# Loading and transposing the prefetched mask tiles earlier in a hand-ordered graph-attention kernel

## The chip, the cores and the metric

The kernel runs on one core of one Trainium2 chip, in one launch. The metric is device time in microseconds (us), as the median of several runs. TensorE (PE) does matmuls and transposes, VectorE (DVE) and ScalarE (ACT) work on whole tiles, GpSimd (POOL) adds tiles and issues the transfers that convert types or add into their destination, SyncE (SP) issues the other transfers. Each engine takes its instructions in the order of the program; an instruction that waits holds those behind it on the same engine.

## The reference, cut to what matters

For each of 16 samples (1024 nodes, 256 features) there are two attention layers over the same adjacency matrix, 4 heads of 64 in the first and 8 heads of 32 in the second:

```python
h = jnp.maximum(_layernorm(x), 0.0)
q, k, v = heads(h @ Wq), heads(h @ Wk), heads(h @ Wv)
scores = einsum('bhnd,bhmd->bhnm', q, k) / sqrt(D)
scores = where(adj > 0, scores, -inf)        # layer 1: adj == 0 gives -inf
x = x + (softmax(scores) @ v).reshape(b, n, e) @ Wo.T + bo
```

`adj` is int32 and has 16 x 1024 x 1024 entries of 0 or 1. The kernel computes scores transposed (keys on the partitions), so it needs the adjacency transposed too.

## The kernel before, in words

**Stream of steps.** Each sample is 16 steps of layer 0 and 32 of layer 1. The stream takes layer 0 of sample b + 1 and then layer 1 of sample b, over and over, so 48 steps bring one sample forward. In what follows `a` is the first step of layer 0 of sample b + 1 and `c` = a + 16 the first of layer 1 of sample b. A step computes four 128x512 blocks of scores (`scores`, L400, TensorE, into two PSUM pairs of which there are three), masks them (`exponentials`, L416, VectorE), exponentiates them (L421, ScalarE), and two steps later (`LEAD`) multiplies them with the values (`weigh`, L433, TensorE). If a step has a large item (keys, queries, values, the output projection), the `weigh` of an even step is put off to the next, and one does both.

**The mask.** `masks[b]` holds the transposed adjacency of a sample as fp8, in two halves of four tiles. A tile t (128 rows of the adjacency) takes three steps of its own:

- `load` (L128): GpSimd issues the transfer of 128x1024 int32 to bf16 into the tile `adj`. This tag has **one** buffer, so a load waits until the flip of the tile before has read it.
- `flip` (L134): SyncE issues a transposing transfer `adj` to `adjT`. That tag has one buffer as well, so a flip waits for the load and for the put of the tile before.
- `put` (L143): ScalarE converts `adjT` to the fp8 mask.

Layer 1 reads the same mask after `second` (L151) has changed its values in place.

**What sets the order.** All work beside the steps is given a due step by hand: `later(i, f, ...)`. Within a step the order is: scores, `weigh`, the counts and GpSimd adds of `count_steps`, the exponentials, the add tiles of layer 0, then the due items in the order in which they were registered, large ones last. The loads, flips and puts are registered before the stream runs, so they come before a spread, an invert or an accumulate that falls due in the same step, as those are registered while it runs.

For the masks of samples 2 to 15 the puts of tiles 0 to 7 are due at a + 7, 12, 17, 22, 33, 37, 41 and 45; tiles 2 to 7 thus fall into layer 1. For `masks[1]` a loop of its own spaces the tiles by two steps in the first layer 0. `masks[0]` goes through staging tiles and isn't touched.

**What GpSimd and SyncE have in layer 1.** The softmax sums of a group of 8 steps are made by adding probability tiles. At each odd step GpSimd adds the tile of the step two back to the one before it (L534, 128x2048, 4.7 us); some of the results are added together by transfers with accumulation (`accumulate`, L520, 1 MB). In program order this gives, on GpSimd:

- a+31: L534; a+33: L520, L534; a+35: L534; a+36: L520; a+37: L534, L520; a+39: L534; a+41: L520, L534; a+43: L534; a+44: L520
- between them: `add_bias` (L198, x<-bo) at a+34 and a+43, the four small instructions of `stats` (L177 to L183) at a+38, `normalize` (L352) at a+42

The probability tiles of odd steps have two buffers: the masking of step i + 2 (VectorE, L416) waits for the L534 of step i, as that one reads the tile to be overwritten.

SyncE has for each group a `spread` (four issues of L333, sums<-s, after ScalarE's copy L320), and an `invert`: one issue of L343 (vd<-vn) and four of L346 (inv<-vd), which wait until L343's transfer has landed. In layer 1 the spread of a group that ended at step i is due at i + 8, the invert at i + 12, the `normalize` at i + 17 in the first half; groups end at a+25 and a+33, so there is a spread at a+33 and a+41 and an invert at a+37 and a+45.

Of the kernel before, what the change touches and what calls it, by code (L numbers as in the profile page):

```python
# [82 lines left out]
def fast_program(ctx, tc, a, w, loads, chk):  # L83
# [375 lines left out]
    class Stream:  # L459
# [12 lines left out]
        def later(self, i, f, *args):  # L472
            self.due.setdefault(i, []).append((f, args))
# [116 lines left out]
    mask, inp = masks[0], inputs[0][0]  # L590
# [74 lines left out]
    later = stream.later  # L665

    def norms(inp, half, *at):

        for i, f in zip(at, (inp.stats, inp.stats, inp.norm, inp.norm)):
            later(i, f, half, (0, 1) if i in (at[0], at[2]) else (2, 3))  # L670
        later(at[3] + 1, inp.add_bias, half)

    def half_inputs(inp, half, *at):

        for i, f in zip(at, (inp.turn, inp.k, inp.q, inp.values)):
            later(i, f, half)
# [3 lines left out]
        later((u - 4) // 2, flip, u)  # L680
        later(u - 1, mask.put, u)
    for t in range(NT):
        i = 6 + 2 * t
        later(i - 3, masks[1].load, t)
        later(i - 2, masks[1].flip, t)
        later(i, masks[1].put, t)
# [5 lines left out]
    for b in range(B - 1):  # L692
        mine, a, c = inputs[1][b], first[b + 1], second[b]
        if b == 0:

            norms(mine, 0, a + 5, a + 6, a + 8, a + 9)
            half_inputs(mine, 0, a + 11, a + 12, a + 14, a + 14)
            norms(mine, 1, a + 13, a + 14, a + 15, c)
            half_inputs(mine, 1, c + 1, c + 3, c + 6, c + 4)
        else:  # L700
            norms(mine, 0, a - 20, a - 19, a - 16, a - 15)
            half_inputs(mine, 0, a - 13, a, a + 2, a + 8)
            norms(mine, 1, a - 14, a - 10, a - 8, a - 6)
            half_inputs(mine, 1, a - 1, c, c + 6, c + 2)
        for i, u in zip((0, 2, 4, 6, 8, 10, 12, 13), range(NT)):
            later(a + i, masks[b].second, u)
        if b + 2 < B:
            other, mask = inputs[0][b + 2], masks[b + 2]
            later(a + 5, open_x, b + 2, 0)
            later(a + 13, open_x, b + 2, 1)  # L710
            if b == 0:
                norms(other, 0, a + 14, a + 15, c + 2, c + 3)
                half_inputs(other, 0, c + 5, c + 8, c + 16, c + 18)
                norms(other, 1, c + 3, c + 4, c + 6, c + 7)
                half_inputs(other, 1, c + 11, c + 22, c + 26, c + 30)
            else:
                norms(other, 0, a + 10, a + 12, a + 13, a + 15)
                half_inputs(other, 0, c + 1, c + 8, c + 16, c + 18)
                norms(other, 1, c, c + 4, c + 5, c + 6)
                half_inputs(other, 1, c + 9, c + 22, c + 26, c + 30)  # L720
            for i, t in zip((7, 12, 17, 22, 33, 37, 41, 45), range(NT)):
                later(a + i - 5 + (t > 4), mask.load, t)
                later(a + i - 2, mask.flip, t)
                later(a + i, mask.put, t)
        else:
            last, e = inputs[1][b + 1], c + 32
            norms(last, 0, c + 5, c + 6, c + 8, c + 9)
            half_inputs(last, 0, c + 11, c + 14, c + 16, c + 20)
            norms(last, 1, c + 13, c + 14, c + 16, c + 17)
            half_inputs(last, 1, c + 19, c + 24, e + 6, e + 4)  # L730
            for u in range(NT):
                later(c + 8 + 2 * u, masks[b + 1].second, u)
# [158 lines left out]
def kernel(  # L891
# [28 lines left out]
    with ExitStack() as fast, tc.manual_schedule():  # L920
        fast_program(fast, tc, a, w, loads, chk)
# [61 lines left out]
```

## Time and profile before

| | |
|---|---|
| median of 3 runs | 3354.03 us (3348.64 to 3355.82) |
| profiled execution | 3351.91 us, its span 3349.8 us |
| busy | PE 3254.1 us (97%), DVE 2530.3 (76%), POOL 2349.8 (70%), ACT 2172.9 (65%) |
| granted TensorE clock | 0.989 |
| transfers that GpSimd issues | q0: 224.42 MB, 37.6% of 16 engines' span |
| transfers that SyncE issues | q1: 104.41 MB, 13.8% |
| load of a mask tile | 256 KB read, 3.9 us to landing (median of 128) |
| flip of a mask tile | 4.1 us to landing (median of 124) |
| accumulate p<-p | 1024 KB, 8.5 us to landing (median of 150) |

How to read it: a line of the costliest groups gives the source line, the engine, the operation, the tiles by name (written <- read), their shapes and the number of instructions; then the busy time in us and the mean ns of one; then the idle time of that engine just before these instructions, and what ended most of it. A line of the waits gives who waited for whom, the total in us, how often, and the longest. A line of a timeline gives the start in us from the start of the span, the duration in us, engine, line, operation and tiles, the count of instructions merged into it, and in brackets the idle time before it and its releaser. Durations of issues on SP and of DMA lines on POOL are those of the issuing, not of the transfer.

### The profile page before, as it was taken

What the parts mean: (1) busy time and instruction counts of PE and PEld (TensorE: products, weight loads), DVE (VectorE), ACT (ScalarE), POOL (GpSimd) and SP (SyncE); (2) the same over time, 40 slices, a digit from 0 to 9 for tenths busy, and PEclk for the clock granted to TensorE, in tenths of its full rate; (3) what the DMA queues carried; (4) which work ended last, traced back from release to release, by engine and by line L of the source; (5) the groups of instructions that cost most, each with busy time, mean ns of one, the idle gap of its engine ahead of it and who ended that gap; (6) DMA issues with size and microseconds to landing.
All of it is one profiled execution on the core that took longest, in us unless ns stands there. A gap on an engine that the chain in (4) does not pass through costs nothing.

```text
span 3349.8 us, 44407 instructions
## 1 busy us (share of the span) xinstructions
PE 3254.1 (97%) x16990; PEld 1274.2 (38%) x16990; DVE 2530.3 (76%) x2760; ACT 2172.9 (65%) x2402; POOL 2349.8 (70%) x1244
## 2 busy tenths in 40 slices
PE   8999999999999999999999999999999999999898
PEld 3343343333334343343434334344343343433333
DVE  5777877778777787776877767777687876778866
ACT  5567576675756757567575766757667576674565
POOL 4578586775857858577686776858668586785766
PEclk9999999999999999999999999999999999999999
DMA  7338265472643827456274563836638365380431
GB/s 142 66 73 148 66 120 102 86 145 64 125 94 81 147 64 139 80 98 127 68 145 79 98 124 65 149 81 107 118 64 151 70 114 108 76 155 26 87 78 31
DMA packets 309453, 331.74 MB, mean 99 GB/s; under 512 B 189552, under 2 KB 257392, under 8 KB 290032
## 3 DMA queue, kind: packets, MB, share of 16 engines
q0 software_dynamic: 73824, 224.42, 37.6%
q1 hardware_dynamic: 235408, 104.41, 13.8%
q8 instruction: 135, 2.21, 0.3%
q14 instruction: 86, 0.70, 0.1%
HBM read 119.54 MB, written 17.56 MB: 41 GB/s over the span
## 4 chain that ended last, share of the span: by engine, by line
PE 81%; DMA 6%; POOL 5%; ACT 4%; DVE 3%; issue 2%; SPq 1%; ACTq 0%; POOLq 0%; DVEq 0%
PE ps L400 27%; PE po L433 25%; PE pq L225 11%; PE py L381 7%; PE pv L262 6%; PE pz L301 4%; POOL p L534 4%; DMA adjT<-adj 3%; ACT p L421 2%; DVE p L416 2%; DMA p<-p 2%; PE ph L208 1%; ACT mask L143 1%; ACT hT L209 0%; ACT s L320 0%
## 5 line engine op out<-in xcount | busy, mean ns | idle before, releaser
L416 DVE SCALAR_TENSOR_TENSOR p<-mask,ps 128x1024 f32<-128x1024 fp8e4 x1536 | 1794.4, 1214 | 646.4 <-PE ps L400 599.3
L421 ACT ACTIVATE p<-p 128x1024 f32<-128x1024 f32 x1536 | 1611.5, 1056 | 871.8 <-DVE p L416 829.8
L534 POOL TENSOR_TENSOR p<-p,p 128x2048 f32<-128x2048 f32 x255 | 1191.2, 4675 | 240.2 <-PE po L433 221.3
L400 PE MATMUL ps<-qT,kT 32*128 32x512 f32 (+1 forms) x6144 | 1165.0, 637 | 12.8 <-DVE p L416 11.3
L433 PE MATMUL po<-p,v 128*32 128x512 f32 (+1 forms) x6144 | 1016.4, 608 | 39.1 <-ACT p L421 38.1
L400 PEld LDWEIGHTS ps<-qT,kT 32*128 32x128 f32 (+1 forms) x6144 | 376.7, 186 | 695.9 <-issue 372.6
L446 POOL TENSOR_TENSOR p<-p 128x1024 f32<-128x1024 f32 x128 | 318.9, 2491 | 299.6 <-DVE p L445 294.6
L433 PEld LDWEIGHTS po<-p,v 128*32 128x32 f32 (+1 forms) x6144 | 231.8, 118 | 744.1 <-issue 515.5
L445 POOL TENSOR_TENSOR p<-p 128x1024 f32<-128x1024 f32 x64 | 151.5, 2368 | 250.2 <-DVE p L442 179.7
L262 PE MATMUL pv<-wv,hT 128*128 128x256 f32 x1024 | 238.9, 387 | 14.5 <-ACT hT L209 14.5
L225 PE MATMUL pq<-hT,wk 128*128 128x512 f32 x512 | 239.0, 610 | 1.5 <-ACT hT L209 1.3
L381 PE MATMUL py<-wo,cat 128*128 128x256 f32 x1008 | 234.9, 386 | 2.2 <-ACT hT L209 1.0
L225 PE MATMUL pq<-hT,wq 128*128 128x512 f32 x512 | 236.6, 605 | 0.1
L262 PEld LDWEIGHTS pv<-wv,hT 128*128 128x128 f32 x1024 | 190.3, 191 | 87.9 <-ACT hT L209 26.8
L381 PEld LDWEIGHTS py<-wo,cat 128*128 128x128 f32 x1008 | 187.5, 191 | 72.7 <-issue 45.5
L143 ACT ACTIVATE mask<-adjT,mhalf 128x1024 fp8e4<-128x1024 bf16 x124 | 140.7, 1136 | 92.7 <-DMA adjT<-adj 92.7
L520 POOL DMA_DIRECT2D p<-p x150 | 151.3, 1008 | 54.2 <-POOL p L534 21.6
L352 POOL TENSOR_TENSOR cat<-cat,inv 128x512 f32<-128x512 f32 x127 | 169.2, 1332 | 8.8 <-DMA inv<-vd 6.2
L301 PE MATMUL pz<-p,ones 128*32 128x512 f32 (+1 forms) x1112 | 172.7, 595 | 0.8 <-ACT s L320 0.8
L448 POOL TENSOR_TENSOR p<-p,p 128x1024 f32<-128x1024 f32 x64 | 156.1, 2439 | 5.0
L442 DVE TENSOR_TENSOR p<-p 128x1024 f32<-128x1024 f32 x128 | 156.0, 1219 | 0.0
L225 PEld LDWEIGHTS pq<-hT,wk 128*128 128x128 f32 x512 | 93.0, 191 | 143.5 <-issue 94.1
(50 smaller groups left out, 1697.2 us busy)
## 6 DMA issues: line engine op xcount, KB each, us to landing
p<-p POOLq DMA_DIRECT2D x150, 1024.0 KB, 8.5
adj<-in_adj_dram POOLq DMA_DIRECT2D x128, 256.0 KB, 3.9
x<-bo POOLq DMA_DIRECT2D x64, 512.0 KB, 5.7
x<-in_x_dram SPq DMA_DIRECT2D x32, 512.0 KB, 4.4
inv<-vd SPq DMA_DIRECT2D x128, 128.0 KB, 2.9
inv<-vd SPq DMA_DIRECT2D x252, 64.0 KB, 2.7
out_dram<-x SPq DMA_DIRECT2D x31, 512.0 KB, 3.0
sums<-s SPq DMA_DIRECT2D x384, 2.0 KB, 1.8
```

Of the source, the lines that this page charges most:

```text
L143: nc.scalar.activation(self.m[qh][:, :, ts(t % 4, P)], self.flipped.pop(t), AF.Identity, bias=w.mhalf[:, 0:1], saturate=False,)
L225: nc.tensor.matmul(pq[:, m, :], wt[self.layer][:, c, ts(m, P)], self.hT[half][:, c, :], start=(c == 0), stop=(c == 1),)
L262: nc.tensor.matmul(pv[:, i, :], self.hT[half][:, c, ts(i, P)], w.v[self.layer][:, c, :], start=(c == 0), stop=(c == 1),)
L301: nc.tensor.matmul(self.s[r * self.D : (r + 1) * self.D, :], w.ones[:, : self.D], p[:, r, :], start=start, stop=stop,)
L352: nc.gpsimd.tensor_mul(o, o, self.inv)
L381: nc.tensor.matmul(py[:, i, :], self.half.cat[:, c, ts(i, P)], w.o[self.layer][:, c, :], start=(c == 0), stop=(c == 1),)
L400: nc.tensor.matmul(st.ps[i // 2][:, i % 2, :], gr.inp.kT[r * D : (r + 1) * D, gr.g, ts(kt, P)], gr.inp.qT[gr.qh][r * D : (r + 1) * D, gr.g ...
L416: nc.vector.scalar_tensor_tensor(out=half, in0=gr.mask.m[gr.qh][:, kt, :].unsqueeze(1).to_broadcast([P, 2, 512]), scalar=BIG, in1=st.ps[i] ...
L421: nc.scalar.activation(half, half, AF.Exp, scale=gr.scale)
L433: nc.tensor.matmul(gr.o[r * D : (r + 1) * D, :], gr.inp.v[:, kt, h * D : (h + 1) * D], st.p[:, i, :], start=(kt == 0), stop=(kt == NT - 1),)
L446: nc.gpsimd.tensor_add(a, a, b)
L534: nc.gpsimd.tensor_add(one, one, st.p)
```

## The change

```diff
     for t in range(NT):
-        i = 6 + 2 * t
+        i = 5 + 2 * t
         later(i - 3, masks[1].load, t)
         later(i - 2, masks[1].flip, t)
         later(i, masks[1].put, t)
...
             for i, t in zip((7, 12, 17, 22, 33, 37, 41, 45), range(NT)):
-                later(a + i - 5 + (t > 4), mask.load, t)
-                later(a + i - 2, mask.flip, t)
+                later(a + i - 6, mask.load, t)
+                later(a + i - 3, mask.flip, t)
                 later(a + i, mask.put, t)
```

In the first loop all three items of each tile of `masks[1]` come one step earlier. In the second, the puts stay where they are. All flips come one step earlier: at a + 4, 9, 14, 19, 30, 34, 38 and 42. The loads of tiles 0 to 4 come one step earlier and those of tiles 5 to 7, which stood four steps ahead of their puts, two: at a + 1, 6, 11, 16, 27, 31, 35 and 39. No instruction is added or removed.

## The prediction

> **What bounds the kernel now.** I read the page first. TensorE is busy for 97% of the span, at a granted clock of 0.989, so the layers' matmuls set most of the time, and a change in the mask's transfers can only win back gaps. The waits say where a mask tile makes one:
>
> ```profile
> L143 ACT ACTIVATE mask<-adjT,mhalf 128x1024 fp8e4<-128x1024 bf16 x124 | 140.7, 1136 | 92.7 <-DMA adjT<-adj 92.7
> ```
> ```profile
> ACT mask L143 <- DMA adjT<-adj: 92.7, 16, 7.7
> POOL adj L128 <- DMA adjT<-adj: 61.3, 15, 5.5
> DVE p L416 <- POOL p L534: 45.9, 41, 4.8
> ```
>
> ScalarE writes 124 tiles but waits in 16 of them. Two of these waits (1.0 and 1.7 us in ScalarE's timeline) lie in the first 75 us. The other 14, (92.7 - 2.7)/14 = 6.4 us each, come once in each of the 14 samples whose masks the main loop prefetches (b + 2 = 2 to 15), and the chain in order of time has an adjT transfer of 6.4 to 9.5 us in every one. I looked at one, from 1718 to 1768 us. The order of the puts shows which tile it is: t = 6, put at a+41. GpSimd's and SyncE's timelines there:
>
> ```profile
> 1718.73 0.92 POOL L520 DMA_DIRECT2D p<-p  x1 [1.79 <-PE po L433]
> ...
> 1723.92 0.84 POOL L128 DMA_DIRECT2D adj<-in_adj_dram  x1
> 1724.52 1.60 POOL L198 DMA_DIRECT2D x<-bo  x1
> 1726.18 4.56 POOL L534 TENSOR_TENSOR p<-p,p 128x2048 f32<-128x2048 f32 x1
> 1730.69 0.88 POOL L520 DMA_DIRECT2D p<-p  x1
> 1731.30 4.87 POOL L534 TENSOR_TENSOR p<-p,p 128x2048 f32<-128x2048 f32 x1
> 1736.47 0.87 POOL L520 DMA_DIRECT2D p<-p  x1 [0.30 <-POOL p L534]
> 1737.05 0.86 POOL L128 DMA_DIRECT2D adj<-in_adj_dram  x1
> ...
> 1739.88 4.56 POOL L534 TENSOR_TENSOR p<-p,p 128x2048 f32<-128x2048 f32 x1
> 1745.19 0.92 POOL L520 DMA_DIRECT2D p<-p  x1 [0.75 <-PE po L433]
> 1745.88 4.79 POOL L534 TENSOR_TENSOR p<-p,p 128x2048 f32<-128x2048 f32 x1
> 1754.50 0.60 POOL L128 DMA_DIRECT2D adj<-in_adj_dram  x1 [3.82 <-DMA adjT<-adj]
> 1755.11 1.29 POOL L352 TENSOR_TENSOR cat<-cat,inv 128x512 f32<-128x512 f32 x1
> 1756.36 4.57 POOL L534 TENSOR_TENSOR p<-p,p 128x2048 f32<-128x2048 f32 x1
> ```
> ```profile
> 1723.23 3.00 SPq L333 DMA_DIRECT2D sums<-s  x4
> 1728.24 2.30 SPq L134 DMA_TRANSPOSE adjT<-adj  x1
> ...
> 1738.93 3.77 SPq L346 DMA_DIRECT2D inv<-vd  x4
> 1746.22 2.05 SPq L134 DMA_TRANSPOSE adjT<-adj  x1
> ```
> ```profile
> 1753.96 1.15 ACT L143 ACTIVATE mask<-adjT,mhalf 128x1024 fp8e4<-128x1024 bf16 x1 [5.71 <-DMA adjT<-adj]
> ```
> ```profile
> 1760.96 2.35 DVE L416 SCALAR_TENSOR_TENSOR p<-mask,ps 128x1024 f32<-128x1024 fp8e4 x2 [4.00 <-POOL p L534]
> ```
>
> Load 6 goes out right behind a 1 MB accumulate (L520, 1736.47) and lands 9.1 us later. Its flip starts at 1746.22, now right behind the next accumulate (1745.19), and takes 7.7 us, to 1753.94. ScalarE was ready for the put at 1748.25. There is one adj buffer, so GpSimd sits in load 7 until the same flip lands, which holds its next two large adds; the second (a+43) ends at 1760.93, and VectorE waits 4.00 us for it. So **two waits end together** here: ScalarE's backlog after the put, and GpSimd's.
>
> **What the Trainium skill says.** (1) "DMA: Bandwidth & Descriptors", section "Issuing engines are not separate DMA queues": transfers issued by SyncE, ScalarE and GpSimd run on the same 16 DMA engines and interleave. The trace agrees: a flip's landing is 3.0 us at least, 4.1 at the median, 12.7 at most, and those issued beside an accumulate take 6 to 9. (2) Same page, "Anatomy of one DMA — SWDGE (gpsimd) path", gives 2.0 us plus bytes over 436 GB/s; for the 256 KB load that makes 2.6 us. The trace has 3.9 at the median, which I use. (3) "Advanced Engine Details and Errata", section "Sequencer and Instruction Queues": an engine instruction waits for its semaphores after it is queued. GpSimd's add behind load 7 shows here what that means: it doesn't start before the load has had its flip.
>
> **The change, part by part.** A sample takes 16 steps of 5.2 us in layer 0 (83.6 us in all) and 32 in layer 1 (122.1 us, 3.8 each; 3.5 between the puts at a+33 and a+37).
>
> *Tiles 0 to 3, and masks[1].* All three waits of tiles 0 to 3 are zero in the 14 samples, and their loads and flips move one step in stretches where GpSimd idles (up to 7.4 us before L446): 0. For masks[1] the whole chain moves one step; its order among the other work changes little, and it may save the 1.7 us wait or cost as much by meeting the first mask's flips: 0, +-2 us.
>
> *Load 4* moves from a+28 to a+27. It already stands directly behind the add of a+27 (1701.45), ahead of the accumulate of a+28, and keeps that place. Flip 4 starts when it lands. 0.
>
> *Load 5* moves two steps, from behind the add of a+33 to behind the one of a+31, into GpSimd's idle 1.79 us before 1718.73. Flip 4 had landed by 1712.4. Cost 0 as its 0.6 us lie in idle time; without that cover, 0.6. *Flip 5* (a+34) then waits no more for the load, but for the four L333 issues ahead of it on SP, which end at 1726.23; it starts 2 us earlier. It lies behind x<-bo (1724.5) only, no longer beside the accumulate of 1730.69, so I give it 4.5 us in place of 6.1: lands 1730.8.
>
> *Load 6* moves from a+37 to a+35. GpSimd reaches it at 1730.74, waits for flip 5 (0 to 1.5 us; I take 0.6, as GpSimd also needed 0.56 after the landing at 1753.94): 1731.4. The accumulate of a+36 moves to 1732.0, the add of a+37 ends at 1737.5, its accumulate goes out at 1737.7, 1.2 late. As load 6 is no longer there (0.6), the add of a+39 ends at 1745.1 instead of 1744.44. VectorE waited for that add already (0.68 us), so step a+41 and with it the put's due time move by 0.65, to 1748.9.
>
> *Flip 6* moves from a+39 to a+38. SP runs it after the invert of a+37, whose L346 issues end at 1742.7: that, not the load, sets its start. It meets the accumulate of 1737.7 in its second half. In this trace a flip behind an accumulate lands 1.1 to 1.2 us after it (1753.94 against 1745.19 + 7.6). With 8.2 to 9 us for that accumulate (it was 8.2), flip 6 lands at **1747.4**. Bounds: 1742.7 + 3.05 = 1745.8 undisturbed, 1742.7 + 7.7 = 1750.4 if it collides as now. At 1747.4 the put doesn't wait: 6.4 us of ScalarE's idle time go, per sample.
>
> *What is late next: load 7.* It moves from a+41 to a+39, now **ahead of** that step pair's accumulate and add. GpSimd is free at 1745.1 and waits for flip 6 until 1748.0. Queued behind it: accumulate, add of a+41, L352, add of a+43. From landing to the end of that last add: 0.56 + 0.6 + 0.7 + 4.79 + 1.25 + 4.57 = 12.5 us, so 1759.9 against 1760.93. Before, only load, L352 and one add (7.0 us) followed the landing. So a landing that comes 6.5 us earlier brings GpSimd 1.0 us. VectorE's a+43 (then at 1754.1 after the add of a+41) and a+44 (4.7 us for both) end at 1758.8, before it; a+45 waits for GpSimd and is 1.0 earlier, then the scores of a+46, which need its PSUM, then the value matmuls of that step. That is the gain of this sample; its ScalarE wait (5.7) is 0.7 below the mean of 6.4, so a mean sample gains about 1.7. Some accumulates will also be slower afterwards; I take 1.5.
>
> *Flip 7* goes after L333 of a+41 and has 10 us until its put: 0.
>
> **Sum.** 14 x 1.5 = 21 us. The profiled execution took 3351.91 (span 3349.8 and 2.1 around it), so 3331 there; it lies 2.1 below the median of the runs, 3354.03, so 3333 as a median. A difference of 0.2% (6.7 us) is about what a measurement of this kernel can tell from no change.
>
> **The rivals.** *GpSimd-limited gain* (above): 0.6 to 2.2 us per sample, 3323 to 3346.
>
> *Full gain.* Flip 6 lands undisturbed at 1745.8; the same 12.5 us give 1758.3, 2.6 us here, 3.3 in a mean sample, and TensorE, which lost 2.0 us outright at 1754.6 and some 2.4 in groups stretched by waits (two of eight po matmuls at 2.0 and 1.9 us instead of 1.07, one of eight ps at 2.0 instead of 1.25), takes all of it: 14 x 2.5 to 3.5 = 35 to 49, so 3305 to 3319. For it: the load no longer stands in the accumulate's way. Against: the accumulate of 1737.7 is surely in flight at 1742.7.
>
> *Nothing in sum.* Flip 6 lands about when it breaks even (below), 3346 to 3360: the gain at the put is given back in GpSimd's queue.
>
> *Slower: load 7 holds GpSimd's adds.* The price of flip 6 landing late is now 12.5 us of queued GpSimd work instead of 7.0. It decides from a landing at 1748.4 in this sample (1749.1 in a mean one), 6.4 us after its issue. If it collides as now (7.3 to 7.7 us), each sample loses about 1.0: 3354 + 14 = 3368. For it: flip 4, issued 3.6 us after an accumulate, takes 6.7. Against: flip 6 comes 5 us after its one, and no transfer of load 6 shares the engines any more.
>
> **Chances.** GpSimd-limited 0.54 (3333), full 0.16 (3312), nothing 0.12 (3353), slower 0.18 (3368). Faster by over 0.2%: the first two, 0.70; same 0.12; slower 0.18. The range reaches over the first three, nearly: 3307 to 3360. The likeliest case's own is 3323 to 3346.
>
> **What would show it.** Right: the wait of mask L143 for adjT falls from 92.7 to under 20 us; the load of tile 6 takes about 4 us in place of 9; GpSimd's wait in L128 stays near 50 us, but stands ahead of the accumulate and add of a+41; VectorE's wait for L534 is split over a+41, a+43 and a+45; the chain's share of adjT falls from 3.2% to below 1% and L534's rises from 3.5%. Wrong: flip 6 lands over 6.4 us after its issue, or SP reaches it later than 6 us after the place where load 6 stood, or L534 waits nowhere for L128 (then the gain is the full one).

## The result and the profile after

The change takes 3352.86 us (median of 12 runs, 3349.33 to 3356.48) against 3350.16 us for the kernel before (12 runs): a ratio of 1.0007, 95% interval 0.9999 to 1.0015. That is no change that this measurement can tell. Forecast were 21 us less. The profiled execution took 3351.93 us, its span 3350.1 us.

The wait that the forecast started from has gone. From the view of the tile `adjT` of the changed kernel (what ScalarE's puts sat idle for: us, times):

```profile
its engine sat idle before it (us, times) until:
  DMA adjT<-adj: 0.5, 2
```

92.7 us of ScalarE's idle time became 0.5, and the span didn't move. The waits of the changed kernel show who took them over (total us, times, longest):

```profile
DVE p L416 <- POOL p L534: 87.1, 63, 3.4
...
POOL adj L128 <- DMA adjT<-adj: 71.3, 27, 4.6
```

GpSimd's wait in the loads rose from 61.3 to 71.3 us and occurs 27 times instead of 15; VectorE's wait for GpSimd's large adds rose from 45.9 to 87.1 us. The same sample as before, GpSimd and then SyncE (start, duration, what, idle time before it):

```profile
1734.70 0.59 POOL L128 DMA_DIRECT2D adj<-in_adj_dram  x1 [1.73 <-DMA adjT<-adj]
1735.29 0.90 POOL L520 DMA_DIRECT2D p<-p  x1
1735.86 4.89 POOL L534 TENSOR_TENSOR p<-p,p 128x2048 f32<-128x2048 f32 x1
1741.06 0.86 POOL L520 DMA_DIRECT2D p<-p  x1 [0.30 <-POOL p L534]
...
1743.89 4.56 POOL L534 TENSOR_TENSOR p<-p,p 128x2048 f32<-128x2048 f32 x1
1751.87 0.66 POOL L128 DMA_DIRECT2D adj<-in_adj_dram  x1 [3.42 <-DMA adjT<-adj]
1752.52 0.92 POOL L520 DMA_DIRECT2D p<-p  x1
1753.12 4.91 POOL L534 TENSOR_TENSOR p<-p,p 128x2048 f32<-128x2048 f32 x1
1757.63 1.61 POOL L352 TENSOR_TENSOR cat<-cat,inv 128x512 f32<-128x512 f32 x1
1758.86 4.90 POOL L534 TENSOR_TENSOR p<-p,p 128x2048 f32<-128x2048 f32 x1
```
```profile
1728.68 3.19 SPq L134 DMA_TRANSPOSE adjT<-adj  x1
1736.08 0.35 SPq L343 DMA_DIRECT2D vd<-vn  x1
1744.01 3.79 SPq L346 DMA_DIRECT2D inv<-vd  x4
1747.96 1.28 SPq L134 DMA_TRANSPOSE adjT<-adj  x1
```

Load 6 (1734.70) waits for flip 5 and holds the accumulate and the add behind it. Load 7 (1751.87) waits for flip 6 and holds an accumulate, two adds and L352. Flip 6 stands behind the four L346, and these wait until vd, issued at 1736.08, has landed at 1743.95, after 7.9 us (the longest of the 13 samples below; 6.6 in the mean). The chain of work through this place runs along exactly these instructions (start, us, what):

```profile
1747.96 3.34 DMA adjT<-adj
...
1751.87 0.66 POOL adj L128
1752.53 0.15 POOL p L520
...
1753.12 3.63 POOL p L534
...
1757.63 1.61 POOL cat L352
1759.24 4.53 POOL p L534
...
1763.79 1.23 DVE p L416
...
1765.06 1.13 PE ps L400 x4
```

Before, the adjT piece led to the put on ScalarE. Now it leads to load 7 on GpSimd.

**Where the time went, step by step.** Both traces hold the same 1536 maskings (L416), two a step, so the start of a step's first L416 can be compared in both. Taken from step a on, mean over the 13 samples b = 1 to 13, after minus before:

| step | after - before, us |
|---|---|
| a+8 | 0.0 |
| a+11 | +1.6 |
| a+16 to a+40 | +0.3 to +0.5 |
| a+41 | +1.5 |
| a+43 | +4.1 |
| a+45 | -0.1 |
| a+48 | -0.1 |

So there are two effects: about 0.4 us **lost** in steps a+8 to a+16 of layer 0, where I had expected nothing, and about 0.5 us **won** between a+40 and a+45, where I had expected 1.5. The second starts with a loss of 3.6 us, from GpSimd's held adds, before the vanished put wait pays it back.

### The profile page after: what moved, and what is told of

Its sections match the earlier page's. It is cut to its first block, busy times and chain, and to the rows that moved or that the text cites. A ratio compares the mean times of both kernels' runs of the same rounds, so it can differ in the third digit from the quotient of the medians.

```text
span 3350.1 us, 44439 instructions
## 1 busy us (share of the span) xinstructions
PE 3264.9 (97%) x16990; PEld 1278.5 (38%) x16990; DVE 2549.1 (76%) x2760; ACT 2180.1 (65%) x2402; POOL 2361.0 (70%) x1244
## 4 chain that ended last, share of the span: by engine, by line
PE 80%; POOL 6%; DMA 4%; DVE 3%; ACT 3%; issue 2%; SPq 1%; POOLq 0%; ACTq 0%; DVEq 0%
PE ps L400 27%; PE po L433 24%; PE pq L225 11%; PE py L381 7%; PE pv L262 7%; POOL p L534 5%; PE pz L301 4%; DVE p L416 3%; DMA adjT<-adj 2%; ACT p L421 1%; PE ph L208 1%; ACT mask L143 1%; DMA vd<-vn 1%; ACT hT L209 1%; POOL cat L352 0%
## 5 line engine op out<-in xcount | busy, mean ns | idle before, releaser
L416 DVE SCALAR_TENSOR_TENSOR p<-mask,ps 128x1024 f32<-128x1024 fp8e4 x1536 | 1790.8, 1213 | 624.0 <-PE ps L400 529.6
L534 POOL TENSOR_TENSOR p<-p,p 128x2048 f32<-128x2048 f32 x255 | 1200.1, 4709 | 253.4 <-PE po L433 234.1
L400 PE MATMUL ps<-qT,kT 32*128 32x512 f32 (+1 forms) x6144 | 1195.8, 636 | 37.2 <-DVE p L416 35.6
L433 PE MATMUL po<-p,v 128*32 128x512 f32 (+1 forms) x6144 | 992.8, 602 | 1.0 <-ACT cat L312 1.0
L446 POOL TENSOR_TENSOR p<-p 128x1024 f32<-128x1024 f32 x128 | 319.4, 2495 | 283.7 <-DVE p L445 278.7
L445 POOL TENSOR_TENSOR p<-p 128x1024 f32<-128x1024 f32 x64 | 151.4, 2366 | 258.9 <-DVE p L442 178.6
L352 POOL TENSOR_TENSOR cat<-cat,inv 128x512 f32<-128x512 f32 x127 | 178.7, 1407 | 7.8 <-DMA inv<-vd 4.9
L151 DVE TENSOR_SCALAR mask<-mask 128x1024 fp8e4<-128x1024 fp8e4 x128 | 169.8, 1326 | 0.0
L448 POOL TENSOR_TENSOR p<-p,p 128x1024 f32<-128x1024 f32 x64 | 152.1, 2377 | 5.0
L225 PEld LDWEIGHTS pq<-hT,wq 128*128 128x128 f32 x512 | 93.4, 192 | 144.1 <-issue 118.4
```

Of the source, the lines that this page charges most:

```text
L151: nc.vector.tensor_scalar(m, m, -0.5, 0.5, op0=ALU.not_equal, op1=ALU.subtract, saturate=False)
L225: nc.tensor.matmul(pq[:, m, :], wt[self.layer][:, c, ts(m, P)], self.hT[half][:, c, :], start=(c == 0), stop=(c == 1),)
L352: nc.gpsimd.tensor_mul(o, o, self.inv)
L400: nc.tensor.matmul(st.ps[i // 2][:, i % 2, :], gr.inp.kT[r * D : (r + 1) * D, gr.g, ts(kt, P)], gr.inp.qT[gr.qh][r * D : (r + 1) * D, gr.g ...
L416: nc.vector.scalar_tensor_tensor(out=half, in0=gr.mask.m[gr.qh][:, kt, :].unsqueeze(1).to_broadcast([P, 2, 512]), scalar=BIG, in1=st.ps[i] ...
L433: nc.tensor.matmul(gr.o[r * D : (r + 1) * D, :], gr.inp.v[:, kt, h * D : (h + 1) * D], st.p[:, i, :], start=(kt == 0), stop=(kt == NT - 1),)
```

## The experiments

All times are beside runs of the kernel before on the same chip (3350 to 3351 us). The table gives means over the 13 samples, read from the traces, in us from the first masking of step a+35 where a time is a point. "vd" is the time from issue to landing of the vd transfer of the invert of a+37. The table comes from one profiled execution of each kernel; that of `e5_mix` took 3329.03 us, 9 us over its median, so part of the difference between its column and the others isn't the edit's. `e1_late` is the change without its early tiles; all are described below.

| | before | change | `e1_late` | `e5_mix` | `e7_acc` | `e8_flip5` | `e9_load6` | `e10_hold` |
|---|---|---|---|---|---|---|---|---|
| load 6 starts | 12.1 | 6.8 | 6.7 | 6.8 | 6.8 | 5.5 | 12.0 | 5.5 |
| GpSimd's wait in load 6 | 0 | 1.2 | 1.1 | 1.2 | 0.5 | 0 | 0 | 0 |
| vd | 4.6 | 6.6 | 7.1 | 7.1 | 6.5 | 6.5 | 4.5 | 6.5 |
| the four L346 end | 17.5 | 19.1 | 19.6 | 19.7 | 19.0 | 18.8 | 17.4 | 18.9 |
| accumulate of a+37 starts | 11.5 | 13.2 | 13.1 | 13.3 | 12.3 | 11.9 | 11.4 | 11.9 |
| accumulate of a+37 lands | 20.0 | 22.0 | 22.0 | 22.0 | 20.9 | 20.6 | 20.0 | 20.6 |
| flip 6 starts | 22.0 | 19.3 | 19.8 | 19.9 | 19.1 | 18.9 | 21.9 | 19.0 |
| flip 6 lands | 29.6 | 23.7 | 23.7 | 23.8 | 22.9 | 22.5 | 29.7 | 22.6 |
| GpSimd's wait in load 7 | 4.1 | 3.7 | 3.7 | 0 | 0 | 0 | 4.2 | 3.8 |
| masking of a+41 | 19.5 | 20.7 | 20.6 | 20.7 | 19.8 | 19.4 | 19.4 | 19.4 |
| masking of a+45 | 36.8 | 36.3 | 36.4 | 34.8 | 33.4 | 33.0 | 36.8 | 35.3 |

### The two parts apart

Tiles 4 to 7 alone:

```diff
-        i = 5 + 2 * t
+        i = 6 + 2 * t
...
-                later(a + i - 6, mask.load, t)
-                later(a + i - 3, mask.flip, t)
+                later(a + i - (6 if t >= 4 else 5), mask.load, t)
+                later(a + i - (3 if t >= 4 else 2), mask.flip, t)
```

> Only tiles 4 to 7 are moved as in the change; tiles 0 to 3 and masks[1] stay where they were. Theory (two effects that cancel: about 0.5 us won per sample in steps a+40 to a+45, about 0.4 lost in steps a+8 to a+16 of layer 0): the loss goes, so 13 to 14 times 0.5 remains, 5 to 8 us less than before, a ratio near 0.998. Rival (the layer-0 difference is chance, and the change as a whole does nothing): ratio 1.000 to 1.001, as with the whole change.

Measured: 3347.51 us, ratio 0.9992 (0.9984 to 1.0000). Half of what was expected, and the interval just reaches 1. Step by step there is nothing left in layer 0 (0.0 at a+16) and -0.3 us remains at a+48.

Tiles 0 to 3 and masks[1] alone:

```diff
-                later(a + i - 6, mask.load, t)
-                later(a + i - 3, mask.flip, t)
+                later(a + i - (6 if t < 4 else 5 - (t > 4)), mask.load, t)
+                later(a + i - (3 if t < 4 else 2), mask.flip, t)
```

> The other part alone: tiles 0 to 3 and masks[1] one step earlier, tiles 4 to 7 as before. Theory: the loss of layer 0 without the gain, 14 x 0.4 = 5 to 6 us more than before, ratio near 1.0017, and VectorE's L151 stays as long as after the change (about 1.33 us at the mean against 1.13). Rival: these tiles had no wait, their move costs nothing, ratio 1.000.

Measured: 3358.83 us, ratio 1.0022 (1.0015 to 1.0029), L151 1345 ns. The early tiles cost some 8 us by themselves: +0.5 us a sample at a+16, and nothing after it but 0.1.

### What the early tiles cost

The views of before and of after the change, around steps a+9 to a+11 of the same sample, show an operation that I had not looked at, `second` (L151), on VectorE, beside GpSimd's adds. Each sample has eight L151; the sixth, of step a+10, takes over 2.5 us in 14 of the 16 samples after the change, in 2 before it. Before:

```profile
1624.45 0.82 DVE L151 TENSOR_SCALAR mask<-mask 128x1024 fp8e4<-128x1024 fp8e4 x1
```
```profile
1622.35 2.37 POOL L446 TENSOR_TENSOR p<-p 128x1024 f32<-128x1024 f32 x1 [5.35 <-DVE p L445]
1624.80 2.69 POOL L448 TENSOR_TENSOR p<-p,p 128x1024 f32<-128x1024 f32 x1
```

After:

```profile
1626.03 2.87 DVE L151 TENSOR_SCALAR mask<-mask 128x1024 fp8e4<-128x1024 fp8e4 x1
```
```profile
1623.56 2.36 POOL L446 TENSOR_TENSOR p<-p 128x1024 f32<-128x1024 f32 x1 [5.33 <-DVE p L445]
1626.00 2.35 POOL L448 TENSOR_TENSOR p<-p,p 128x1024 f32<-128x1024 f32 x1
```

Before, L151 starts 0.35 us ahead of L448 and takes 0.82 us, and L448 is the longer for it (2.69 instead of 2.35). After, L448 starts 0.03 us ahead of L151, and L151 lasts until 0.55 us after L448's end. Load 1 (0.6 us of issuing) had stood between GpSimd's adds of step a+7 and its L352. When it moved to a+6, L352 ended 0.6 us earlier counted from step a, and so did VectorE's four small L247 before step a+9 (in both traces they end 0.5 us after L352); L445 and GpSimd's L446 followed them. One load put back tests this:

```diff
-                later(a + i - 6, mask.load, t)
+                later(a + i - (5 if t == 1 else 6), mask.load, t)
```

> The change, but tile 1's load alone back at a+7, its flip staying at a+9. Theory (the layer-0 loss comes from this load: without its 0.6 us in front, GpSimd's two adds of step a+9 start 0.6 us earlier, and the second begins just ahead of VectorE's L151, which then waits until it ends): VectorE's L151 is back at 1.13 us at the mean (1.33 after the change) and the time is 5 to 6 us below the change's, 3346 to 3348. Rival (the flips, which now stand ahead of spreads, inverts and x transfers on SyncE, are the cause): L151 stays at 1.33 and the time at 3352 or more.

Measured: 3349.45 us, ratio 0.9996 (0.9988 to 1.0005). L151 is back at 1133 ns, and the step comparison shows 0.0 us lost at a+16. The time came down by 3 us of the expected 5 to 6 and its interval reaches to 1.0005, so the mechanism is shown by the trace rather than by the time; `e2_early` (8 us) and the pair `e3_load7` and `e5_mix` below (7 us, by the ratios) give the size of the early tiles' loss.

### Load 7, the hold on GpSimd

```diff
-                later(a + i - 6, mask.load, t)
+                later(a + i - (4 if t == 7 else 6), mask.load, t)
```

> The change, but tile 7's load stays at a+41, behind that step's accumulate and add. Theory (the gain of the vanished put wait is given back because load 7 now holds the accumulate and two adds of GpSimd until flip 6 lands): load 7 then finds flip 6 landed, L534 of a+43 ends some 2.6 us earlier per sample, 14 x 2.6 = 36 us less than after the change, about 3315, ratio 0.990. Rival (VectorE and TensorE were the limit behind the put anyway, or tile 7 comes late now and ScalarE waits in its put instead): 3345 or more, ratio 0.998 to 1.003.

Measured: 3328.17 us, ratio 0.9930 (0.9917 to 0.9942). The direction is the theory's, the size two thirds of it: GpSimd's wait in the loads falls from 71.3 to 21.0 us. But the add of a+43, which the masking of a+45 waits for in all 13 samples, ends 1.2 us earlier than in the change, not 2.6. The add of a+41 starts 2.1 us earlier; load 7 now stands between the two adds, and there it takes back about 1 us.

Without the early tiles (this and `e1_late` together; `e5_mix` in the table):

> Tiles 0 to 3 and masks[1] as before the change; tiles 4 to 7 as in the change, but tile 7's load at a+41. Theory (the two causes are separate and add): the gain of tile 7's late load (23 us) and the loss of the early tiles left out (5 to 6 us more), about 3322, ratio 0.991 to 0.992. Rival (they aren't additive): 3328 or more.

Measured: 3319.79 us, ratio 0.9909 (0.9893 to 0.9924). The two causes add.

### Flip 6, ahead of the invert

```diff
-                later(a + i - 3, mask.flip, t)
+                later(a + i - (4 if t == 6 else 3), mask.flip, t)
```

> The change, but tile 6's flip comes at a+37, so that SyncE issues it ahead of the invert of that step instead of behind its four L346. Theory (flip 6 lands late only because SyncE holds it until vd has landed): flip 6 starts some 6 to 8 us earlier, load 7 no longer waits in GpSimd (3.4 us now), about 3 us less per sample, 14 x 3 = 42 us, about 3310, ratio 0.988. Rival (the invert behind the flip makes inv and with it the normalize of a+42 late, which holds GpSimd in its turn; or flip 6 waits for the put of tile 5): 3340 or more, and GpSimd's wait for inv grows from 5 to over 20 us.

Measured: 3392.82 us, ratio 1.0118 (1.0102 to 1.0134). My theory was wrong and the rival right. Flip 6 does start 8.0 us earlier and load 7's wait in GpSimd is gone (0.1 us), but the vd transfer now waits behind the flip on SyncE; it goes out 4.9 us later and takes 9.2 us. From SyncE's and GpSimd's timelines of this run:

```profile
1344.92 2.11 SPq L134 DMA_TRANSPOSE adjT<-adj  x1
1347.12 1.72 SPq L343 DMA_DIRECT2D vd<-vn  x1
1356.42 1.72 SPq L346 DMA_DIRECT2D inv<-vd  x4
```
```profile
1357.22 4.87 POOL L534 TENSOR_TENSOR p<-p,p 128x2048 f32<-128x2048 f32 x1
1364.69 1.28 POOL L352 TENSOR_TENSOR cat<-cat,inv 128x512 f32<-128x512 f32 x1 [2.60 <-PE ps L400]
1365.93 4.52 POOL L534 TENSOR_TENSOR p<-p,p 128x2048 f32<-128x2048 f32 x1
```

inv goes out at 1356.42 and the last of its four transfers lands at 1364.53; L352, which multiplies with it, starts at 1364.69, 2.6 us after the add ahead of it. The bracket names TensorE, but its instruction there isn't what L352 reads; over the whole run the wait of L352 for inv is 29.3 us in 11 times (4.9 in the change). So L352 holds GpSimd's next add in place of load 7, and a sample loses 2.7 us.

### Load 6 and vd

Why did the L346 end 1.6 us later than before the change, when nothing on SyncE was put ahead of them? The first theory was the accumulate of a+36, which load 6's wait moves next to the vd transfer. `behind` registers tile 6's load only at a+34, so that it comes after that accumulate in the order of a+36; the rest is as in `e5_mix`:

```diff
-                later(a + i - (4 if t == 7 else 6 if t >= 4 else 5), mask.load, t)
+                if t == 6:
+                    later(a + i - 7, behind, a + i - 5, mask.load, t)
+                else:
+                    later(a + i - (4 if t == 7 else 6 if t >= 4 else 5), mask.load, t)
```

> As the mix of the other run (tile 7's load at a+41, early tiles as before), with tile 6's load one place later on GpSimd: behind the accumulate of a+36 instead of ahead of it. Theory (the vd transfer takes 6.6 us in place of 4.6 because load 6, waiting for flip 5, moved that accumulate next to it): vd lands in about 4.6 us again, SyncE's L346 end 1.5 to 2 us earlier, and the add of a+37 is held 0.6 us less, about 3314 to 3318. Rival (vd is slow because of other traffic): vd stays over 6 us, or load 6 behind the accumulate takes 9 us again and the put waits: 3322 or more.

Measured: 3308.27 us, ratio 0.9878 (0.9863 to 0.9894). Faster than expected, but the theory of vd fell: the accumulate is back at its old place (5.5 us after step a+35, as before), and vd still takes 6.5 us. What the table shows of the further 11.5 us against `e5_mix` is the shorter wait in load 6 (0.5 in place of 1.2 us) with the accumulate no longer behind it, and a+41 0.9 us earlier. What the kernels with a slow vd have in common is load 6 itself in the stretch before vd: it reads 128x1024 int32, 512 KB, and writes half of that as bf16 (the 256 KB that the table of before calls read are what it writes). Load 6 back at a+37 tests it, in a kernel that has flip 5 early (next run) and no other difference from it:

> The fastest version so far (flip 5 at a+33, load 7 at a+41, early tiles as before) with tile 6's load alone back at a+37. Theory (vd takes 6.5 us in place of 4.6 because load 6 now stands in front of it, wherever the accumulate is): vd lands in 4.6 us again and SyncE's L346 end near 17.5 us after step a+35, as before the change; load 6, behind an accumulate again, takes 9 to 10 us, so the put waits again and the time is within 10 us of the kernel before, about 3345. Rival (vd is slow for another reason, such as flip 5 or load 5 earlier): vd stays over 6 us.

Measured: 3351.90 us, ratio 1.0005 (0.9996 to 1.0013). vd takes 4.5 us again, the L346 end at 17.4, load 6 takes 9.9 us behind its accumulate, and the put wait is back (94.2 us in 15 times). So the 2 us of vd are the price of load 6 standing in front of it, and load 6's place is what the gain of the fast versions rests on. That the later end of the L346 also makes flip 6 land later isn't shown by this: the section on why the prediction was wrong comes back to it.

### Flip 5, ahead of the spread

```diff
-                later(a + i - (3 if t >= 4 else 2), mask.flip, t)
+                later(a + i - (4 if t == 5 else 3 if t >= 4 else 2), mask.flip, t)
```

> As the mix, with tile 5's flip at a+33, ahead of that step's four L333 on SyncE instead of behind them. Theory (load 6 holds GpSimd's accumulate and add of a+37 by 1.2 us per sample until flip 5 has landed): flip 5 lands before GpSimd gets to load 6, that wait falls from 1.2 to below 0.3, step a+41 is 1 us earlier, some 13 us less than the mix, about 3309. Rival (flip 5 must wait for the put of tile 4, and the L333 behind it make the sums and the invert late): 3320 or more.

Measured: 3301.59 us, ratio 0.9856 (0.9841 to 0.9871), the fastest version. That is 18 us less than `e5_mix`, where 13 were expected. Flip 5 goes out 5.4 us earlier than in `e5_mix`, GpSimd doesn't wait in load 6, and a+41 is 1.3 us earlier. GpSimd's timeline, with the two loads in it and no wait for a flip in front of either:

```profile
1703.33 0.59 POOL L128 DMA_DIRECT2D adj<-in_adj_dram  x1
1703.92 0.91 POOL L520 DMA_DIRECT2D p<-p  x1
1704.49 4.90 POOL L534 TENSOR_TENSOR p<-p,p 128x2048 f32<-128x2048 f32 x1
...
1719.51 4.83 POOL L534 TENSOR_TENSOR p<-p,p 128x2048 f32<-128x2048 f32 x1
1724.00 0.86 POOL L128 DMA_DIRECT2D adj<-in_adj_dram  x1
1724.62 1.56 POOL L352 TENSOR_TENSOR cat<-cat,inv 128x512 f32<-128x512 f32 x1
1725.87 4.82 POOL L534 TENSOR_TENSOR p<-p,p 128x2048 f32<-128x2048 f32 x1
```

### The hold alone, in the fastest version

Tile 7's load back at a+39, all else as in `e8_flip5`:

> The fastest version so far with tile 7's load alone at a+39, as in the change. Theory (load 7 holds an accumulate and two adds of GpSimd until flip 6 has landed): GpSimd waits 3 us or more per sample in load 7, the step a+43 comes about 2 us later and the step a+45 about 1.3 to 2 us later than without, 18 to 28 us in all: 3320 to 3330. Rival (with flip 5 early, flip 6 lands so early that the hold costs nothing): within 5 us of 3302.

Measured: 3333.03 us, ratio 0.9948 (0.9932 to 0.9965). Load 7 at a+39 costs 31 us against `e8_flip5`, 2.2 us a sample, although flip 6 lands as early in both (22.6 and 22.5). Its waits:

```profile
DVE p L416 <- POOL p L534: 65.7, 59, 3.4
...
POOL adj L128 <- DMA adjT<-adj: 55.5, 15, 4.6
```

In `e8_flip5` VectorE's wait for L534 is 38.0 us and GpSimd's wait for adjT in L128 is 2.6 us.

The same run answers a second question, as it differs from `e1_late` in one thing only: flip 5 comes at a+33 instead of a+34. Load 7 holds GpSimd in both. The waits of `e1_late`:

```profile
DVE p L416 <- POOL p L534: 77.0, 58, 3.4
...
POOL adj L128 <- DMA adjT<-adj: 68.8, 26, 4.6
```

There GpSimd waits in both loads (26 times); in `e10_hold` the wait in load 6 is gone and the one in load 7 is left (15 times). `e1_late` takes 3347.51 us (ratio 0.9992), `e10_hold` 3333.03 (0.9948). So the wait in load 6, with what it delays, costs some 14 us, 1 us a sample. Without it, and without the early tiles, the change brings 17 us against the kernel before, where 21 were forecast.

## Why the prediction was wrong, step by step

**What bounds the kernel now** was right: the put wait was there, 6.4 us a sample, and SyncE, GpSimd and the accumulates made it as described.

**Load 4, load 5, flip 7**: right; none of their places shows a difference in the step comparison. Flip 5 was put 0.6 us too early: 1730.8 is 5.6 us after step a+35, and it landed at 6.2 in the mean. GpSimd reached load 6 at 5.6, as expected, so its wait grew by the same 0.6.

**"Tiles 0 to 3, and masks[1] ... 0"** failed. They cost 0.4 to 0.5 us a sample in the traces; the times, with their noise, give 5 to 8 us in all. I had looked at the waits of these tiles and at GpSimd's idle time and found both free. The cover that I named, GpSimd's idle time, was real; but an engine that comes to its next work earlier can be in another engine's way. The loads decided which of L151 and L448 starts first. The Trainium skill says this of the two engines ("SBUF — State Buffer", section "Who interferes with whom": a VectorE operation in a two-port mode and a GpSimd operation share a port pair, and the one that issues first has it for its whole instruction while the other blocks). The trace agrees on the order: L151 takes 0.82 us when it is first, 2.87 when it is second by 0.03 us. That L151 runs in such a mode no run here shows.

**"Load 6 ... waits for flip 5 (0 to 1.5 us; I take 0.6)"** and, built on it, **"flip 6 lands at 1747.4"** are the terms of the sum that failed. The mechanism was right, the sizes were not. Load 6 waited 1.2 us. The accumulate of a+37 behind it went out 13.2 us after step a+35, where my 1737.7 is 12.5, took 8.8 us, and flip 6 landed 1.7 us after it, where I had read 1.1 to 1.2 from the trace of before. So flip 6 landed at 23.7 in the mean, where my 1747.4 is 22.2, and a+41 came 1.1 us later in place of 0.65. The pair `e1_late` and `e10_hold` puts a time on it: without load 6's wait the accumulate lands at 20.6, flip 6 at 22.6, and some 14 us come back.

**"SP runs it after the invert of a+37, whose L346 issues end at 1742.7: that, not the load, sets its start"** was right in the order and wrong in the time. I took the 1742.7 over from the trace of before, as if the change could not move it. The L346 wait for vd; load 6, moved into the stretch before vd, made it 6.6 us instead of 4.6, and the L346 ended 1.6 us later. So one of my signs of being wrong came true: SyncE reached flip 6 7.2 us after the place where load 6 had stood, and 6 was my limit. But the traces don't show that this late start set the landing. In `e6_load1` the L346 end at 18.3, in `e5_mix` at 19.7, and flip 6 lands at 23.8 in both, with the accumulate of a+37 landing at 22.4 and 22.0. In `e8_flip5` and `e10_hold` the L346 still end at 18.8 to 18.9, and flip 6 lands 1.2 us earlier than in the change, as the accumulate does by 1.4. Over the 104 flips 6 of the eight kernels in which load 6 is early and flip 6 stays behind the invert, the landing has a correlation of 0.81 with the landing of the accumulate of a+37 and of -0.17 with the flip's own start. So it was the accumulate, and not the L346, that the landing went with. No run has load 6 early and vd as short as before, so a smaller share of the L346 stays open.

**"What is late next: load 7"** was the right mechanism: 12.5 us of queued work follow the landing instead of 7.0 (in the sample shown 1751.30 to 1763.76, 12.5). With a break-even near 1749.1 in a mean sample (23.9 on this scale), the 1.5 us that flip 6 came late took nearly all of the 1.5 us of gain; 0.3 to 0.5 us were left. `e10_hold`, where flip 6 lands near the forecast 22.2 (22.6), has the forecast gain: its a+45 comes 1.5 us earlier than before the change.

**Sum.** 14 samples with about 0.5 won and 0.4 to 0.5 lost give zero within two microseconds. The measured 3352.86 us lies inside my range, but by another case than the one I held likeliest. The rival "nothing in sum" (0.12) is what happened, half by its own mechanism, and half by one that I had not named. My sum was right on where the wait would go and overrated what would be left: 12.5 us of queued work followed a landing that I knew to 2 us at best.

## What to carry to other kernels

A transfer issued earlier also stands earlier in front of the work behind it on its engine: with one buffer, a load that waited for its buffer held everything behind it in its engine's queue here (12.5 us of work behind load 7). Moving load 6, load 7 and flip 6 earlier each only moved the wait. It went away when the waiting instruction was put *behind* the work that had to pass (load 7 in `e3_load7`), or when what it waited for came earlier (flip 5 in `e8_flip5`). When a step is moved, the times of other transfers in the stretch that it moves into can't be taken over from the old trace (here vd went from 4.6 to 6.6 us, and the accumulate of a+37 started 1.7 us later). And before costing a move at nothing because the engine idles, look at what runs on the other engines in the stretch where its next work will now begin.

## What the runs showed of the hardware that I had not expected

- A VectorE fp8 `tensor_scalar` of 128x1024 takes 0.82 us, or 2.87 us when it comes 0.03 us after the start of a GpSimd add of 2.35 us.
- A transfer of a few KB to DRAM (vd) lands in 1.4 us at the median in layer 0 (4 KB). In layer 1 (8 KB) that of the invert of a+37 lands in 4.6 us, 3 us behind the issue of a 1 MB accumulate, and in 6.0 to 7.1 us, by the kernel, with a mask tile's load in the stretch before it as well.
- In the kernel before, flip 6 went out 1.5 us after an accumulate and landed 1.2 us after it. In the kernels with load 6 early it went out 5 to 7 us after one, and landed 1.4 to 2.0 us after it.
- Moving a single load by two steps (load 7, `e10_hold` against `e8_flip5`) is worth 31 us, 0.9% of the kernel, with not one transfer or operation more or less.
